# Seven-product projections of a two-layer attention kernel: the fourteen products of a pair in another order

## The chip, the cores and the metric

The kernel runs on one core of a Trainium2 chip. A core has a matrix engine (TensorE, PE in the profile), a vector engine (VectorE, DVE), a scalar engine (ScalarE, ACT), a general engine (GpSimd, POOL) and a queue that issues transfers (SyncE, SP). Each engine works through its own list of instructions in order, and semaphores tie the lists together. Matrix products land in PSUM, a memory of eight banks; a bank holds 512 fp32 values in each of 128 partitions. The metric is the device time of one execution in microseconds (us).

## The reference

Two residual layers run one after the other on `x` of shape 1 x 128 x 256 x 256 (row, position, channel), all in fp32. The part that the change concerns is the four projections of layer 0: q, k, v and the gate, each a product of every row (256 positions x 256 channels) with a 256 x 256 matrix.

```python
# layer 0: x = x + attention(group_norm(x)), for each of 128 rows s, 8 heads of 32 channels
bias = einsum('nijz,zh->nhij', pair_repr, bias_proj)
gate = sigmoid(msa @ gate_proj)
q, k, v = split(msa @ qkv_proj, 3)
sim = softmax(einsum('nsqhc,nskhc->nshqk', q, k) / sqrt(32)) + bias
out = (einsum('nshqk,nskhc->nsqhc', sim, v) * gate) @ out_proj
# layer 1: x = x + banded_attention(group_norm(x)), 4 heads of 64 channels, |i - j| <= 16,
# with biases on its input and output projections
```

## The kernel before

A first stage loads `x` for the statistics of the group norm and turns the pair bias. Layer 0 then goes row by row over `s` from 0 to 128, with the instructions of TensorE, ScalarE and VectorE in exactly the order in which the program text calls them. Layer 1 follows, and the change doesn't touch it.

**Seven products for two rows.** Two neighbouring rows (pair `i`) are projected together. A projection of two rows by a 256 x 256 matrix is a 2 x 2 by 2 x 2 product of blocks of 128, which takes eight block products, or seven with sums of blocks formed beforehand. The kernel uses seven. The sums of weight blocks (`sums_q` and so on) are made once. The sums of input blocks (`ts`) are made on POOL for each pair by `sum_rows`. The class `Seven` (lines 589 to 631) holds one projection: `ps` is its bank in PSUM, with two halves of 256 columns; `to` is the result in SBUF; `mid` holds two partial results.

- Products 1, 6, 7 and 4 go into half 0 of the bank one after the other and add up there, so the half is read between them: after 1, after 6, after 7 and after 4.
- Products 5 and 3 add up in half 1, which is read after 5 and after 3 (the last reading takes both halves, after 3 and 4).
- Product 2 goes to another bank, `twos`, which the two projections of a stretch share.

Each reading is a copy by ScalarE, in `take`: "15" (both halves, 512 columns, line 621), "6" (half 0, 256 columns, line 623), "7" (half 0, line 625) and "34" (both halves, line 627). The copy of `twos` (512 columns, line 756) is the ninth of a stretch. POOL adds the parts together in `add` (lines 630 and 631). On TensorE, q, k and g are products of 256 columns at line 610, v is two products of 128 columns at line 614. Every fp32 product is recorded as two matmuls and two weight loads (four of each for v).

**The stretch.** `stretch(names, i)` does the fourteen products of two projections, f and g: "qk" in even rows and "vg" in odd rows. In the text below, f6 is product 6 of f, and so on. The order on TensorE before is

f1 f5 g1 g5 f2 g2 f6 g6 f3 g3 f7 g7 f4 g4

and the order of the copies on ScalarE is

f15 g15 f6 g6 twos f7 g7 f34 g34.

A product into a bank waits until the last copy out of this bank has ended. A copy waits for the last product into its bank that stands ahead of it in the program.

**Around the stretch.** In a row the order on TensorE is: scores of the first four heads (`sim`, line 640), sums of the heads' weights of the row before (`zs`, 681), products with the bias (`bv`, 667), scores of the other four heads, products `av` of the row before (667), the stretch, and the output projection `po` of the row before (513). `po` waits for `at`, which VectorE computes from `av`, the reciprocal `d` and `bv` (lines 697 to 715). ScalarE takes the exponentials `ex` of the scores (651) and the copies. The banks of `ps`, `twos`, `po` and the scores come from one ring of five.

Of the kernel before, what the change touches and what calls it, by code (L numbers as in the profile page):

```python
# [9 lines left out]
F32 = mybir.dt.float32  # L10
# [5 lines left out]
P = 128  # L16
R = 256
# [22 lines left out]
def conv_preact_kernel(  # L40
# [31 lines left out]
    def bank(which, name):  # L72
        pool, tag, bufs = ring[which]
        return pool.tile([P, 2, R], F32, tag=tag, name=name, bufs=bufs)

    def proj_bank(name):
        return bank("proj", name)
# [461 lines left out]
    with ExitStack() as both:  # L539
# [11 lines left out]
        with ExitStack() as lay0:  # L551
            row = lay0.enter_context(tc.tile_pool(name="row0", bufs=2))
# [179 lines left out]
            def stretch(names, i):  # L732

                if 2 * i >= S:
                    return
                f, g = (Seven(w, i) for w in names)

                f.open()
                f.product(1)
                f.product(5)  # L740
                g.open()
                g.product(1)
                g.product(5)
                f.take("15")
                twos = proj_bank(f"p2{names}{i}")
                f.product(2, twos[:, 0, :])
                g.product(2, twos[:, 1, :])
                g.take("15")
                f.product(6)
                g.product(6)  # L750
                f.take("6")
                f.product(3)
                g.product(3)
                g.take("6")
                two = row.tile([P, 2, R], F32, tag="two", name=f"two{names}{i}")
                nc.scalar.copy(two, twos)  # L756
                f.product(7)
                g.product(7)
                f.take("7")
                g.take("7")  # L760
                f.product(4)
                g.product(4)
                f.take("34")
                g.take("34")
                for n, p in enumerate((f, g)):
                    p.add(two[:, n, :])


            with tc.manual_schedule(engines={mybir.EngineType.PE, mybir.EngineType.Activation, mybir.EngineType.DVE}):
                for s in range(2):  # L770
                    normal(s)
                sum_rows(0)
                stretch("qk", 0)
                for s in range(2, 4):
                    normal(s)
                stretch("vg", 0)
                sum_rows(1)
                for s in range(S + 1):
                    if s < S:
                        scores(s, 0)  # L780
                    zs = sum_heads(s - 1)
                    join_tiles(s, 0, 0)
                    divide(s - 1, zs)
                    if s % 2 == 0 and s < S:
                        e = res["g", s // 2]
                        nc.scalar.activation(e, e, AF.Exp, scale=-1.0)
                    if s < S:
                        scores(s, 1)
                    z = hd[s - 1, "z"][0] if s > 0 else None
                    attend(s - 1)  # L790
                    for half, j in ((0, 2), (1, 0), (1, 2)):
                        join_tiles(s, half, j)
                    least(s - 1, z)
                    if s == S - 1:
                        most1 = join_most(st1, stats1, 1)
                        load1(0)
                        load1(1)
                    stretch(("qk", "vg")[s % 2], s // 2 + 1)
                    normal(s + 4)
                    if s % 2 == 1:  # L800
                        sum_rows((s + 3) // 2)
                    if s > 0:
                        finish(s - 1, by_channel(out_sb, 0, st[s - 1]["at"], f"po{s - 1}"))
# [6 lines left out]
        with ExitStack() as lay:  # L810
            ps_av = psum(lay, "1", 4, 0)
            row = lay.enter_context(tc.tile_pool(name="row1", bufs=4))
# [186 lines left out]
    with tc.If(sure < P):  # L999
        with ExitStack() as lay:  # L1000
            one = lay.enter_context(tc.tile_pool(name="one2", bufs=1))
            two = lay.enter_context(tc.tile_pool(name="two2", bufs=2))
# [174 lines left out]
```

## Time and profile before

| | |
|---|---|
| time, median of 3 runs | 3417.53 us (3411.97 to 3417.85) |
| span of the profiled execution | 3410.0 us |
| TensorE clock granted | 0.992 |
| TensorE matmuls busy | 3292.2 us |
| TensorE weight loads busy | 2476.5 us |
| VectorE busy | 2554.7 us |
| ScalarE busy | 1781.7 us |
| POOL busy | 1140.2 us |
| layer 0's first product, first scores, last output projection | at 193.1, 208.9 and 2228.8 us |
| stretches in layer 0 | 64 "qk" and 64 "vg" |

Layer 0 is thus some 2030 us of the span, or about 15.8 us for a row. Busy times are sums of the lengths of records. Records of matmuls overlap, since a matmul begins before the one before it has ended, so that a busy TensorE is not one that never waits. A weight load (PEld) is recorded by itself and normally runs while the product before it is still at work. In a line of the timeline, the columns are the start, the length, the engine, the line of the kernel, the operation, output and inputs by name, shapes and count; what stands in brackets at the end is how long the engine was idle before it, and what ended that.

### The profile page before, as it was taken

The page shows a single profiled execution, that of the slowest core. Times are in us where ns is not written, and L with a number is a line of the kernel's source. Part 1 is how long each engine was busy: PE and PEld are TensorE (multiplying, and loading weights), DVE is VectorE, ACT ScalarE, POOL GpSimd, SP SyncE. Part 2 cuts the span into 40 slices and gives each one's busy share as a digit, 9 for nine tenths or more (in the row PEclk, how much of TensorE's full clock was granted, in tenths as well). Part 3 has the DMA queues.
Part 4 walks back from the last instruction along what each step waited for, and adds up shares of the span by engine and source line. Part 5 has one row for each costly group of instructions (what it writes and reads, how often), then busy time and mean ns, then how long its engine had stood idle before and what let it go on. Part 6 is the DMA issues. An engine that isn't in the chain of part 4 may idle for free.

```text
span 3410.0 us, 86688 instructions
## 1 busy us (share of the span) xinstructions
PE 3292.2 (97%) x37193; PEld 2476.5 (73%) x37193; DVE 2554.7 (75%) x3794; ACT 1781.7 (52%) x3866; POOL 1140.2 (33%) x1135
## 2 busy tenths in 40 slices
PE   6799999999999999999999999989999999999997
PEld 4466666666666666666666666678888888888886
DVE  4747777787787777778778777757777777777777
ACT  4565555555555556555565555534444444444442
POOL 3033333333333333333333333223333333333332
PEclk9999999999999999999999999999999999999999
DMA  9921111111111111111111111002222222222221
GB/s 383 411 59 52 48 35 32 38 32 32 39 32 38 32 37 33 32 38 32 32 39 32 39 32 32 20 20 64 54 61 64 64 61 54 64 64 63 54 61 46
DMA packets 346328, 209.36 MB, mean 61 GB/s; under 512 B 273608, under 2 KB 339152, under 8 KB 339664
## 3 DMA queue, kind: packets, MB, share of 16 engines
q1 hardware_dynamic: 345040, 201.37, 20.2%
q8 instruction: 294, 4.82, 0.6%
q0 software_dynamic: 752, 2.36, 0.2%
q14 instruction: 98, 0.80, 0.1%
q10 hardware_dynamic: 144, 0.00, 0.0%
HBM read 136.59 MB, written 67.11 MB: 60 GB/s over the span
## 4 chain that ended last, share of the span: by engine, by line
PE 87%; ACT 5%; DMA 3%; DVE 3%; issue 1%; SPq 0%; ACTq 0%; POOL 0%; DVEq 0%
PE sim L640 8%; PE p1v L841 7%; PE av L667 7%; PE 1po L513 7%; PE p1q L513 7%; PE p1k L513 7%; PE po L513 6%; PE bv L667 6%; PE pv L614 6%; PE pq L610 5%; PE pk L610 4%; PE zs L681 4%; DMA xs<-in_x_dram 3%; PE pg L610 3%; PE 1sim L862 3%; PE 1avz L894 2%
## 5 line engine op out<-in xcount | busy, mean ns | idle before, releaser
L651 ACT ACTIVATE ex<-sim 128x512 f32<-128x512 f32 x1024 | 528.8, 603 | 362.9 <-PE sim L640 362.9
L919 DVE RECIPROCAL 1rz<-1z 128x512 f32<-128x512 f32 x128 | 427.6, 3341 | 174.2 <-ACT 1z L917 174.2
L872 POOL TENSOR_TENSOR 1p<-1ex,seen 128x768 f32<-128x768 f32 x128 | 233.4, 1824 | 737.4 <-ACT 1ex L870 737.4
L697 DVE RECIPROCAL d<-d 128x512 f32<-128x512 f32 x128 | 429.2, 3353 | 4.3
L657 DVE TENSOR_TENSOR both<-ex 128x512 f32<-128x512 f32 x512 | 332.8, 690 | 121.4 <-ACT ex L651 121.3
L640 PE MATMUL sim<-q,k 32*128 32x256 f32 x4096 | 294.9, 400 | 1.2 <-ACT ex L651 1.2
L630 POOL TENSOR_TENSOR v<-v,twovg 128x256 f32<-128x256 f32 x64 | 46.6, 728 | 735.7 <-ACT twovg L756 735.7
L833 ACT ACTIVATE 1q<-p1q,bqk 128x256 f32<-128x256 f32 x256 | 107.5, 471 | 345.2 <-PE p1q L513 345.2
L640 PEld LDWEIGHTS sim<-q,k 32*128 32x128 f32 x4096 | 186.2, 184 | 102.3 <-issue 92.8
L513 PE MATMUL po<-at,out_sb 128*128 128x256 f32 x1024 | 245.4, 383 | 12.1 <-DVE at L715 12.1
L667 PE MATMUL av<-ex,v 128*32 128x256 f32 x4096 | 247.5, 382 | 0.0
L513 PE MATMUL 1po<-1at,w_out_t 128*128 128x256 f32 x1024 | 241.9, 389 | 5.1 <-DVE 1at L921 5.1
L513 PE MATMUL p1q<-xn,w_in_t 128*128 128x256 f32 x1024 | 244.1, 381 | 2.0 <-DVE xn L493 1.1
L667 PE MATMUL bv<-bias_sb,v 128*32 128x256 f32 x4096 | 244.5, 379 | 0.0
L513 PE MATMUL p1k<-xn,w_in_t 128*128 128x256 f32 x1024 | 243.2, 381 | 0.0
L841 PE MATMUL p1v<-w_in_t,xn 128*64 128x128 f32 x4096 | 237.9, 274 | 0.0
L841 PEld LDWEIGHTS p1v<-w_in_t,xn 128*64 128x64 f32 x4096 | 222.2, 137 | 21.6 <-issue 21.6
L513 PEld LDWEIGHTS 1po<-1at,w_out_t 128*128 128x128 f32 x1024 | 191.3, 192 | 54.5 <-ACT 1z L917 23.9
L723 DVE TENSOR_TENSOR o<-po,xt 128x512 f32<-128x512 f32 x128 | 88.5, 692 | 187.1 <-PE po L513 186.9
L513 PEld LDWEIGHTS po<-at,out_sb 128*128 128x128 f32 x1024 | 196.4, 192 | 40.6 <-issue 7.7
L630 POOL TENSOR_TENSOR q<-q,twoqk 128x256 f32<-128x256 f32 x64 | 46.6, 728 | 525.3 <-ACT twoqk L756 525.3
L513 PEld LDWEIGHTS p1q<-xn,w_in_t 128*128 128x128 f32 x1024 | 195.3, 191 | 29.4 <-issue 1.3
(226 smaller groups left out, 6722.2 us busy)
## 6 DMA issues: line engine op xcount, KB each, us to landing
pr<-in_L_conv_pair_repr_dram SPq DMA_DIRECT2D x32, 1024.0 KB, 23.0
x<-o SPq DMA_DIRECT2D x64, 512.0 KB, 2.8
yg<-x SPq DMA_DIRECT2D x64, 512.0 KB, 4.2
out_dram<-1o SPq DMA_DIRECT2D x256, 128.0 KB, 4.0
xg<-in_x_dram SPq DMA_DIRECT2D x252, 128.0 KB, 3.2
xs<-in_x_dram SPq DMA_DIRECT2D x15, 2048.0 KB, 21.7
xs<-in_x_dram SPq DMA_DIRECT2D x2, 1024.0 KB, 17.8
qkv_sb<-in_L_conv_qkv_proj_dram POOLq DMA_DIRECT2D x4, 192.0 KB, 12.7
```

What stands on the lines that cost most here:

```text
L513: nc.tensor.matmul(ps[:, m, :], lhsT=w[:, kt, col + m * P : col + (m + 1) * P], rhs=xn[:, kt, :], start=(kt == 0), stop=(kt == 1),)
L610: nc.tensor.matmul(out, lhsT=stationary(self.w, n), rhs=moving, start=first, **flags)
L614: nc.tensor.matmul(out[:, cols], lhsT=moving[:, cols], rhs=stationary(self.w, n), start=first and t2 == 0, **flags)
L640: nc.tensor.matmul(sims[j][:, kt, :], lhsT=k[p0 : p0 + D0, 2 * r + half, kt * P : (kt + 1) * P], rhs=q[p0 : p0 + D0, 2 * r + half, :], sta ...
L651: nc.scalar.activation(ex[:, j], sims[j], AF.Exp, scale=1.0 / math.sqrt(D0))
L657: nc.vector.tensor_tensor(both[:, j : j + 2], ex[:, j : j + 2, 0, :], ex[:, j : j + 2, 1, :], ALU.add)
L667: nc.tensor.matmul(to[D0 * j : D0 * (j + 1), half, :], lhsT=v[:, 2 * r + half, c0 : c0 + D0], rhs=weights(4 * half + j, kt), start=(kt == ...
L681: nc.tensor.matmul(zs[D0 * j : D0 * (j + 1), half, :], lhsT=ones[:, 0:D0], rhs=both[:, j, :], start=True, stop=True,)
L697: nc.vector.reciprocal(d, d)
L841: nc.tensor.matmul(ps[KB * half : KB * (half + 1), b, :], lhsT=xn[:, kt, KB * b : KB * (b + 1)], rhs=w_in_t[:, kt, 2 * C + P * half : 2 * ...
L872: nc.gpsimd.tensor_tensor(p.rearrange("p j (r c) -> p (j r) c", c=WROW)[:, :, 0 : 2 * WSTEP] .rearrange("p r (t c) -> p r t c", c=WSTEP)[: ...
L919: nc.vector.reciprocal(rz, z)
```

## The change

The order of the products and copies within a stretch is changed. Product 3 of each projection goes ahead of product 6, and every copy stands right behind the product whose result it reads. The copy of the twos moves ahead of the copies of product 6, and its tile in SBUF is allocated earlier. The products themselves, the copies, the banks and the additions stay as they are. The order on TensorE after is

f1 f5 g1 g5 f2 g2 f3 f6 g3 g6 f7 g7 f4 g4

and the copies on ScalarE are in the order

f15 g15 twos f6 g6 f7 g7 f34 g34.

It is for this: a copy no longer waits for a product that it doesn't read, and product 3 no longer waits for the copy of product 6, which reads the other half of its bank.

```diff
                 f, g = (Seven(w, i) for w in names)
 
-                f.open()
-                f.product(1)
-                f.product(5)
-                g.open()
-                g.product(1)
-                g.product(5)
-                f.take("15")
+
+                for p in (f, g):
+                    p.open()
+                    p.product(1)
+                    p.product(5)
+                    p.take("15")
                 twos = proj_bank(f"p2{names}{i}")
+                two = row.tile([P, 2, R], F32, tag="two", name=f"two{names}{i}")
                 f.product(2, twos[:, 0, :])
                 g.product(2, twos[:, 1, :])
-                g.take("15")
-                f.product(6)
-                g.product(6)
-                f.take("6")
-                f.product(3)
-                g.product(3)
-                g.take("6")
-                two = row.tile([P, 2, R], F32, tag="two", name=f"two{names}{i}")
                 nc.scalar.copy(two, twos)
-                f.product(7)
-                g.product(7)
-                f.take("7")
-                g.take("7")
-                f.product(4)
-                g.product(4)
-                f.take("34")
-                g.take("34")
+                for p in (f, g):
+                    p.product(3)
+                    p.product(6)
+                    p.take("6")
+                for p in (f, g):
+                    p.product(7)
+                    p.take("7")
+                for p in (f, g):
+                    p.product(4)
+                    p.take("34")
                 for n, p in enumerate((f, g)):
                     p.add(two[:, n, :])
```

## Prediction

> **What bounds the kernel now.** I read the page first: busy shares, then the chain that ended last.
>
> ```profile
> PE 3292.2 (97%) x37193; PEld 2476.5 (73%) x37193; DVE 2554.7 (75%) x3794; ACT 1781.7 (52%) x3866; POOL 1140.2 (33%) x1135
> ...
> PE 87%; ACT 5%; DMA 3%; DVE 3%; issue 1%; SPq 0%; ACTq 0%; POOL 0%; DVEq 0%
> ```
>
> TensorE holds 87% of the chain. Its 97% busy doesn't say that nothing is left: records of matmuls overlap, so short waits hide under them. The record of the weight loads (PEld) has gaps there. The waits of that queue, by what ended them, were read next (us in total, times, longest):
>
> ```profile
> PEld pq L610 <- issue: 34.6, 66, 0.5
> ...
> PEld pv L614 <- ACT midv L623: 31.3, 64, 0.8
> PEld pv L614 <- ACT midv L625: 29.9, 64, 0.5
> PEld pq L610 <- ACT midq L623: 27.6, 64, 0.4
> PEld pk L610 <- ACT midk L623: 27.6, 64, 0.4
> ...
> PEld pg L610 <- ACT midg L623: 17.1, 64, 0.6
> ```
>
> Six groups of about 64, one for each stretch, all in the function under change; 168 us gross. Last I read the timeline of one "qk" stretch, f = q and g = k (start, length; x2 is one product, which is recorded as two matmuls):
>
> ```profile
> 1508.45 0.59 PE L610 MATMUL pq<-ts,sums_q 128*128 128x256 f32 x2
> ...
> 1508.88 0.59 PE L610 MATMUL pk<-ts,sums_k 128*128 128x256 f32 x2
> 1509.08 0.37 ACT L623 COPY midq<-pq 128x256 f32<-128x256 f32 x1 [0.71 <-PE pq L610]
> ...
> 1509.51 0.70 PE L610 MATMUL pq<-xn,sums_q 128*128 128x256 f32 x2
> ...
> 1510.04 0.59 PE L610 MATMUL pk<-xn,sums_k 128*128 128x256 f32 x2
> ...
> 1510.47 0.59 PE L610 MATMUL pq<-ts,sums_q 128*128 128x256 f32 x2
> 1510.67 0.37 ACT L623 COPY midk<-pk 128x256 f32<-128x256 f32 x1 [1.22 <-PE pk L610]
> 1510.94 0.59 ACT L756 COPY twoqk<-p2qk 128x512 f32<-128x512 f32 x1
> ...
> 1511.10 0.70 PE L610 MATMUL pk<-ts,sums_k 128*128 128x256 f32 x2
> 1511.42 0.39 ACT L625 COPY midq<-pq 128x256 f32<-128x256 f32 x1
> ...
> 1511.96 0.67 PE L610 MATMUL pq<-ts,sums_q 128*128 128x256 f32 x2 [0.16 <-ACT midq L625]
> ```
>
> These are f6, g6, (copy of f6), f3, g3, f7, (copy of g6, copy of the twos), g7, (copy of f7), f4. The copy of g6 starts only at 1510.67, right after g3 and long after g6: it stands behind g3 in the program and waits for it.
>
> **Prices from this timeline.** Undisturbed products start 0.433 us apart (1506.29, 1506.72, 1507.16, 1507.59). A copy starts 0.63 after the product it waits for (1508.45 to 1509.08); it takes 0.37, the copy of a product 7 of f 0.39, one of 512 columns 0.59, and the next copy can start 0.10 to 0.12 before that ends (1510.94 to 1511.42). A product held by a copy really starts 0.16 after the copy's end: 1509.45 to 1509.61, where I put its start 0.10 later than recorded because its record is 0.70 long and not 0.59. A held product with a second wait (POOL) starts 0.23 after it (1511.81 to 1512.04). So a turn of product, copy, next product in the same bank needs 0.63 + 0.37 + 0.16 = 1.16, for f4 1.25. One product in between gives 0.87: a stall of 0.30. Two give 1.30: none.
>
> **What the Trainium skill says.** "PSUM — Partial Sum Buffer", section "PSUM bank collisions raise a hardware error": guard by bank and quadrant, not by address. The trace agrees: f3 writes the other half of the bank than the copy of f6 reads, and still starts 0.06 after that copy ends. So moving 3 ahead of 6 removes a wait that the bank, not the data, imposes. "ScalarE: Activation LUTs", section "What ACT_TABLE_LOAD costs": 186 ns + 0.833 ns per column, neighbours overlapping by 93 ns; 399 and 613 ns for 256 and 512 columns, against 372 and 586 to 592 here; I use the trace's. "Perfetto Trace Analysis", section "Identifying Dependency Chains": a second wait may become an instruction of its own ahead; the 0.23 against 0.16 is its price here.
>
> **The change, part by part.** It adds no instruction and removes none: 14 products and 9 copies stay. Before, the waits cost in a qk stretch: f3 for the copy of f6, 0.30; g7 for the copy of g6, which started after g3 (g3, f7, g7 leave 0.87 of 1.16), 0.30; f4 for the copy of f7, held on ScalarE by the copies of g6 and the twos (1511.42 where the product alone would allow 1511.10), 0.41. Sum 1.01. Check: f1 starts at 1505.86, the projection po at 1512.89, 7.03, less 14 x 0.433 = 6.06, leaves 0.97. The vg stretch at 1016.96 to 1024.13: 7.17 less 14 x 0.437 leaves 1.05.
>
> After, f1 at 0: f5 0.43, g1 0.87, g5 1.30, f2 1.73, g2 2.17, f3 2.60, f6 3.03, g3 3.46, g6 3.90. The build's order of waits shows f3 and g3 waiting for the copies of f5 and g5 alone, which end at 0.43 + 0.63 + 0.59 = 1.65 and 2.52: no stall. The copy of the twos now runs from 2.80 to 3.39 and is out of ScalarE's way when the copy of f6 starts at 3.66 (to 4.03). f7, with two waits, could start at 4.26 and has its slot at 4.33: no stall, with 0.07 in hand. Copy of g6 4.53 to 4.90, g7 at 5.06 for a slot at 4.76: stall 0.30. Copy of f7 4.96 to 5.35, f4 at 5.58 for a slot at 5.49: 0.09. Copy of g7 5.69 to 6.06, g4 at 6.22 for 6.01: 0.21. po at 6.65. So 0.60 is left and 0.38 to 0.39 gained. The same sum for vg, where the copies of product 6 start 0.07 later (two waits) and v4 has one, gives po at 6.75: 0.42 gained. 64 x (0.385 + 0.42) = 51.5 us.
>
> Behind these products on TensorE stand po and the next row's scores, and nobody else is queued. The scores reuse the banks of f, g and twos; the last copy ends at 7.4 and they start at po + 1.82 = 8.5. The earlier additions on POOL cost nothing: POOL is 33% busy and q, k feed the row after next. Whether VectorE keeps up is shown by a row without a stretch near the end, where po waits for it:
>
> ```profile
> 2198.01 1.93 PE L667 MATMUL av<-ex,v 128*32 128x256 f32 x32
> 2203.32 1.97 PE L513 MATMUL po<-at,out_sb 128*128 128x256 f32 x8 [3.38 <-DVE at L715]
> ```
>
> VectorE has `at` ready 5.3 us after the products av begin; with a stretch po comes after 9.0 now (1503.89 to 1512.89) and 8.6 then. 3.3 us of slack remain, so the gain isn't given back there.
>
> Unknown: the hand-over to f7 has only 0.07 in hand, and the prices carry some 0.05 each. If each of f7, g7, f4, g4 took 0.05 more, a stretch loses 0.2, 128 x 0.2 = 26 us: 3392. If the copies started or ended enough sooner to shorten g7's and g4's turns by 0.07 each, 18 us more are gained: 3348. I take the sum as worked out.
>
> **Rivals.**
> 1. Part of the gain is lost: f7 misses its slot as it did before (0.15), and VectorE or POOL, whose operations now overlap others, take 0.05. 0.2 of 0.4 is left, 26 us: 3392. For it: f7's small margin. Against: the slack of 3.3 us.
> 2. Nothing changes: the wait moves from f3 to f7 whole. Then f7 would stall by 0.4, so the copy of f6 would have to come 0.4 late; ScalarE is idle for 0.27 before it. 3417.
> 3. All waits go, 1.01 x 128 = 129 us: 3288. Against: g7 and g4 still have only one product between.
> 4. Slower: had f3 to wait for the copy of the twos too, which now stands ahead of it on ScalarE's queue, it would start at 3.55 and not 2.60; 0.95 - 0.40 lost, 128 x 0.55 = 70 us: 3488. For it: that copy was moved forward and every wait on ScalarE counts its instructions in order. Against: the build gives f3 the count of the copy of f5, two copies earlier. A lower clock under denser work is the other way to lose; layer 1 has PEld busy 493 of 560 us at clock 0.99, layer 0 535 of 794 at 1.00, so no.
>
> **How the numbers follow.** Forecast 0.80, rival 1 0.08, 2 0.03, 3 0.03, 4 with the clock 0.06. Time 3417.5 - 51.5 = 3366. The range 3346 to 3390 takes both ends of the unknown prices. Faster by over 0.2%: 0.80 + 0.08 + 0.03 = 0.91; same 0.03; slower 0.06.
>
> **What would show it.** Right: the waits of weight loads for midq and midv at product 3 (31.3 and 27.6 us) gone; the waits before g7 stay near 0.4 each in the record; new ones of the same size before g4; none, or below 0.1, before f7; the copy of the twos directly ahead of the copy of f6; f1 to po 6.6 to 6.8 us. Wrong: f7's load waiting for midq in every stretch, or po waiting for `at`.

## The result, and the profile after

The changed kernel takes 3362.49 us (median of 4 runs, 3361.67 to 3366.80); the kernel before took 3414.81 us beside it (4 runs, 3411.97 to 3417.85). The ratio is 0.9849, with a 95% interval of 0.9832 to 0.9866: 52 us gained, where 51.5 was forecast. The profiled execution spans 3361.1 us against 3410.0.

Busy time of the engines and the shares of the chain that ended last, from the page of the changed kernel:

```profile
PE 3268.2 (97%) x37193; PEld 2493.9 (74%) x37193; DVE 2685.3 (80%) x3794; ACT 1818.2 (54%) x3866; POOL 1254.2 (37%) x1135
...
PE 92%; DMA 4%; DVE 2%; ACT 1%; issue 0%; ACTq 0%; SPq 0%; POOL 0%; DVEq 0%
```

The same number of instructions, and the same 97% for TensorE: that share tells nothing of what happened, as it told nothing of the waits before. What changed is the chain. ScalarE held 5% of it and holds 1%: TensorE's path leads over fewer copies. Two numbers went the wrong way. VectorE is busy 131 us longer (2554.7 before) and POOL 114 us (1140.2), with as many instructions as before. The forecast had neither; its rival 1 names an overlap, at 0.05 us a stretch. It is taken up below. ScalarE's 37 us more (1781.7 before) are not longer copies: those of 256 columns take 372 to 374 ns (372 to 390 before), those of 512 columns 585 to 588 (586 to 593). A busy time here counts overlapping records once, so it is less than the sum of their lengths, and the copies of the stretches now overlap less.

The waits of the weight-load queue in the changed kernel (us in total, times, longest):

```profile
PEld pk L610 <- ACT midk L623: 27.6, 64, 0.4
...
PEld pk L610 <- ACT midk L625: 23.5, 64, 0.4
...
PEld pg L610 <- ACT midg L623: 16.8, 64, 0.3
...
PEld pg L610 <- ACT midg L625: 13.3, 64, 0.2
PEld pq L610 <- issue: 12.9, 64, 0.3
```

Of the six groups shown of before, the copies of f6 (midq and midv at line 623, 27.6 and 31.3 us) no longer hold a product, nor does the copy of v7 (midv at 625, 29.9). The copies of g6 (midk and midg at 623) hold g7 as before, 27.6 and 16.8 against 27.6 and 17.1. The group put down to "issue", which holds f4 in qk, fell from 34.6 to 12.9. New are the copies of g7 (midk at 625, 23.5, and midg at 625, 13.3), which hold g4. No copy holds f7.

One qk stretch of the changed kernel, from its timeline (start, length; x2 is one product), in the order f6, copy of the twos, g3, POOL's first addition, copy of f6, g6, f7, copy of g6, g7, copy of f7, f4, copy of g7, g4, and `po` behind:

```profile
1508.54 0.59 ACT L748 COPY twoqk<-p2qk 128x512 f32<-128x512 f32 x1 [0.28 <-PE p2qk L610]
...
1508.77 0.59 PE L610 MATMUL pq<-ts,sums_q 128*128 128x256 f32 x2
...
1509.20 0.59 PE L610 MATMUL pk<-xn,sums_k 128*128 128x256 f32 x2
1509.20 1.15 POOL L630 TENSOR_TENSOR q<-q,twoqk 128x256 f32<-128x256 f32 x1 [4.90 <-ACT twoqk L748]
1509.40 0.37 ACT L623 COPY midq<-pq 128x256 f32<-128x256 f32 x1 [0.28 <-PE pq L610]
...
1509.63 0.59 PE L610 MATMUL pk<-ts,sums_k 128*128 128x256 f32 x2
...
1510.07 0.59 PE L610 MATMUL pq<-ts,sums_q 128*128 128x256 f32 x2
1510.27 0.37 ACT L623 COPY midk<-pk 128x256 f32<-128x256 f32 x1 [0.49 <-PE pk L610]
...
1510.69 0.70 PE L610 MATMUL pk<-ts,sums_k 128*128 128x256 f32 x2
1510.70 0.37 ACT L625 COPY midq<-pq 128x256 f32<-128x256 f32 x1
...
1511.23 0.66 PE L610 MATMUL pq<-ts,sums_q 128*128 128x256 f32 x2
1511.43 0.37 ACT L625 COPY midk<-pk 128x256 f32<-128x256 f32 x1 [0.36 <-PE pk L610]
...
1511.85 0.70 PE L610 MATMUL pk<-ts,sums_k 128*128 128x256 f32 x2
...
1512.39 0.38 PE L513 MATMUL po<-at,out_sb 128*128 128x256 f32 x1
```

Read it as turns. The copy of f6 starts 0.63 after f6 and ends at 1509.77; f7 starts at 1510.07, in its own slot, 0.44 after g6. The copy of g6 ends at 1510.64 and g7 starts 0.16 after it in truth (1510.80; its record of 0.70 begins 0.10 early), 0.30 behind its slot. g4 follows the copy of g7 in the same way. f1 starts in truth at 1505.74, `po` at 1512.39: 6.65 us, as worked out. In vg it is 6.77 (6.75 worked out).

From `po` to the f1 of the next stretch it is 8.57 us before (1512.89 to 1521.46 recorded) and after (1512.39 to 1520.95: 8.56), so nothing is given back there. Two rows, from one f1 of qk to the next, take 31.54 us before and 30.74 after (median over layer 0); 0.795 x 64 = 51 us. Layer 1 takes nearly the same (its products from first to last `po` 1114.4 and 1115.6 us).

### The profile page after: what moved, and what is told of

The parts are those of the page before. It is cut to its first block, busy times and chain, and to the rows that moved or that the text cites. A ratio compares the mean times of both kernels' runs of the same rounds, so it can differ in the third digit from the quotient of the medians.

```text
span 3361.1 us, 86626 instructions
## 1 busy us (share of the span) xinstructions
PE 3268.2 (97%) x37193; PEld 2493.9 (74%) x37193; DVE 2685.3 (80%) x3794; ACT 1818.2 (54%) x3866; POOL 1254.2 (37%) x1135
## 4 chain that ended last, share of the span: by engine, by line
PE 92%; DMA 4%; DVE 2%; ACT 1%; issue 0%; ACTq 0%; SPq 0%; POOL 0%; DVEq 0%
PE sim L640 8%; PE p1v L835 7%; PE av L667 7%; PE 1po L513 7%; PE po L513 7%; PE p1q L513 7%; PE p1k L513 7%; PE bv L667 6%; PE pg L610 6%; PE pk L610 6%; PE pq L610 5%; PE pv L614 5%; PE zs L681 4%; PE 1sim L856 3%; PE 1avz L888 2%; DMA xs<-in_x_dram 2%
## 5 line engine op out<-in xcount | busy, mean ns | idle before, releaser
L657 DVE TENSOR_TENSOR both<-ex 128x512 f32<-128x512 f32 x512 | 463.1, 944 | 113.0 <-ACT ex L651 113.0
L630 POOL TENSOR_TENSOR v<-v,twovg 128x256 f32<-128x256 f32 x64 | 56.7, 886 | 592.8 <-ACT twovg L748 592.8
L513 PEld LDWEIGHTS p1k<-xn,w_in_t 128*128 128x128 f32 x1024 | 194.6, 190 | 26.5
L493 DVE TENSOR_SCALAR xn<-yg,mean,rstd 128x256 f32<-128x256 f32 x256 | 94.0, 410 | 138.7 <-PE p1v L835 138.7
```

The source lines that it names most:

```text
L513: nc.tensor.matmul(ps[:, m, :], lhsT=w[:, kt, col + m * P : col + (m + 1) * P], rhs=xn[:, kt, :], start=(kt == 0), stop=(kt == 1),)
L657: nc.vector.tensor_tensor(both[:, j : j + 2], ex[:, j : j + 2, 0, :], ex[:, j : j + 2, 1, :], ALU.add)
```

## The experiments

Theory: all that the stretch loses are the turns product, copy, next product in the same bank, as the prediction summed them; so any other order can be summed in the same way, and work placed inside a slack turn is free. Rivals: one half of the change does all of it; VectorE, POOL or something else outside the stretch limits what can be gained; the gain hangs on how much work ScalarE does and not on where it stands. Each kernel was timed in 5 rounds beside the kernel before. That took 3417.80 us beside the two parts of the change, both fillers and the swapped additions, 3416.73 beside the extra copies, one filler and POOL in order, and 3417.55 beside both fillers with POOL in order and the changed kernel run again, which took 3363.85 (ratio 0.9843, 0.9829 to 0.9856). Diffs are against the changed kernel unless the text says otherwise. No kernel leaves out any of the computation.

Lengths from f1 to `po` hardly vary within a run (a few vg stretches take up to 0.3 us longer), so they are read from one stretch. Two places outside the stretches do vary between executions: the first microseconds of layer 0, and the rows behind its last stretch, of which more at the end. From the `po` of the last stretch to the last `po` these rows take 40.6 us in the profile of the changed kernel, 42.0 in that of the same kernel run again, and 43.3 in four of the kernels below.

### Parts of the change alone

Copies moved, product 3 still behind product 6:

```diff
                 for p in (f, g):
-                    p.product(3)
                     p.product(6)
                     p.take("6")
+                for p in (f, g):
+                    p.product(3)
```

> The copies alone are moved: product 6 stays ahead of 3 as in the kernel before, and every copy stands right behind its product, the copy of the twos behind g2. Theory (every stall is a turn of product, copy, next product of 1.16 us less the slots of the products in between): in qk f3 stalls 0.35, f4 0.39, g3, g7 and g4 not, f1 to po is 6.8 us; in vg 6.78; 0.24 and 0.39 a stretch gained over the kernel before, 40 us in all, 3375. Rival 1 (the wait of product 3 that the bank imposes is what counts): f3 still waits, so the time is that of the kernel before, 3415. Rival 2 (the late release of the copy of g6 is all): 3362.

Measured: 3375.73 us, ratio 0.9877 (0.9862 to 0.9892), a gain of 42. f1 to `po` 6.76 in qk (1511.90 to 1518.66) and 6.79 in vg. Its waits show which turn is left:

```profile
PEld pq L610 <- ACT midq L623: 31.2, 64, 0.5
PEld pv L614 <- ACT midv L623: 31.0, 64, 0.5
PEld pq L610 <- POOL k L630: 30.1, 61, 0.5
PEld pv L614 <- ACT midv L625: 27.4, 64, 0.4
```

f3 again waits for the copy of f6, and pays for it; f4 waits for the copy of f7. In qk the record puts f4's wait down to POOL's addition, which ends 0.06 later than that copy. But f4 starts in truth 0.23 after the end of the copy (1517.81 and 1517.58), as it did in the kernel before, so the copy is what it waits for. g3 and g7 now have enough between.

The other part, product 3 ahead of 6, with the copy of the twos behind the copies of product 6 as before:

```diff
-                nc.scalar.copy(two, twos)
                 for p in (f, g):
                     p.product(3)
                     p.product(6)
                     p.take("6")
+                nc.scalar.copy(two, twos)
```

> Product 3 goes ahead of 6 as in the changed kernel, but the copy of the twos stays behind the copies of product 6 as in the kernel before. Theory: the copy of the twos holds the copy of f7 by 0.3 on ScalarE, f4 stalls 0.4 in place of 0.09 and g4 then no longer 0.2; f1 to po is 6.75 in qk and 6.78 in vg against 6.65 and 6.77 in the changed kernel; 6 us slower than it, 3369. Rival (the early copy of the twos is a large part of the gain): half of the gain gone, 3390.

Measured: 3374.17 us, ratio 0.9870 (0.9855 to 0.9886), a gain of 44; f1 to `po` 6.74 and 6.82. The stretches of a pair are 0.14 longer than in the changed kernel, 9 us in all, or 3371. The other 3 us, and so most of the miss against the 3369 written down, lie behind the last stretch in the profile: 43.3 us against 40.6. From its timeline, the copy of the twos, g7, the copies of f7 and g7, and f4:

```profile
1516.04 0.59 ACT L752 COPY twoqk<-p2qk 128x512 f32<-128x512 f32 x1
1516.20 0.70 PE L610 MATMUL pk<-ts,sums_k 128*128 128x256 f32 x2
1516.52 0.39 ACT L625 COPY midq<-pq 128x256 f32<-128x256 f32 x1
1516.93 0.37 ACT L625 COPY midk<-pk 128x256 f32<-128x256 f32 x1
1517.05 0.67 PE L610 MATMUL pq<-ts,sums_q 128*128 128x256 f32 x2 [0.16 <-ACT midq L625]
```

f7 started at 1515.57, so its copy could have begun at 1516.20; the twos ahead of it on ScalarE hold it until 1516.52, and f4 pays. So neither part is the change: they gain 42 and 44 us, and the whole 54. The two gains can't be added, for the parts aren't disjoint: in both, the copies, but for that of the twos in the second, stand right behind their products. The copies as they stood before, with product 3 ahead, weren't run. That saved stalls don't add up is seen from the second part to the whole change, where the products stand in the same order. f4's stall falls from 0.40 to under 0.1, but g4, which did not wait, now stalls by 0.22, and only 0.10 is gained in qk. A stall gives a later turn time for free, and saving it lets the later one appear.

### The same added work in two places

If the sum of turns is right, a copy more on ScalarE costs a full turn where the next product waits, and nothing where there is slack. An extra copy of 256 columns was added ahead of the copy of product 6, first for g (k and g), then for f (q and v); its target is overwritten later.

```diff
                     elif what == "6":
+                        if self.w in "kg":
+                            nc.scalar.copy(self.to[:, 2, :], self.ps[:, 1, :])
                         nc.scalar.copy(self.mid[:, 0, :], self.ps[:, 0, :])
```

> The changed kernel with one more copy of 256 columns on ScalarE in every stretch, right ahead of the copy of g6 and from the same bank (its result is overwritten later). The copy of g6, and with it the turn from g6 to g7, gets 0.27 us longer in qk and 0.21 in vg. Theory: g7 already waits for this turn, so the whole delay reaches the end of the stretch (f1 to po 6.92 in place of 6.65 in qk): 128 x 0.24 = 31 us slower than the changed kernel, 3393. Rival (ScalarE is 54% busy and has room for it): 3362.

Measured: 3397.54 us, ratio 0.9945 (0.9930 to 0.9959), 34 us over the changed kernel. The extra copy (line 624), the copies of g6 and f7, and g7:

```profile
1501.66 0.37 ACT L624 COPY k<-pk 128x256 f32<-128x256 f32 x1 [0.49 <-PE pk L610]
1501.92 0.38 ACT L625 COPY midk<-pk 128x256 f32<-128x256 f32 x1
1502.19 0.39 ACT L627 COPY midq<-pq 128x256 f32<-128x256 f32 x1
...
1502.36 0.70 PE L610 MATMUL pk<-ts,sums_k 128*128 128x256 f32 x2 [0.30 <-ACT midk L625]
```

A copy adds 0.26 here, since neighbours overlap, and g7 waits that much longer. The stretches are 0.27 (qk) and 0.22 (vg) longer than in the changed kernel: 31 us over 64 pairs, as expected. The other 3 lie behind the last stretch (43.3 us against 40.6).

The same copy for f, as a diff against the kernel above:

```diff
-                        if self.w in "kg":
+                        if self.w in "qv":
```

> The same extra copy, but ahead of the copy of f6. The turn from f6 to f7 becomes longer than its three slots, and f7 starts 0.2 us late. Theory: the end of the stretch is set by g6, g7 and g4, whose turns don't begin later for it: f7's delay uses up the time that g7 waits anyway, f4 starts 0.18 later and g4 then has its 0.2 of waiting filled; f1 to po stays 6.65: 3362, within 0.3%. Rival (every longer copy costs what it adds, or f7's 0.2 stays): 25 to 31 us slower, 3387 to 3393.

Measured: 3367.27 us, ratio 0.9856 (0.9840 to 0.9872): 3 to 5 us over the changed kernel's medians, with intervals that overlap. Two rows take 30.74 us, as in the changed kernel. The extra copy, the copy of f6, f7, the copy of g6, and g7:

```profile
1509.19 0.37 ACT L624 COPY q<-pq 128x256 f32<-128x256 f32 x1 [0.28 <-PE pq L610]
...
1509.46 0.38 ACT L625 COPY midq<-pq 128x256 f32<-128x256 f32 x1
1509.98 0.67 PE L610 MATMUL pq<-ts,sums_q 128*128 128x256 f32 x2
1510.06 0.37 ACT L625 COPY midk<-pk 128x256 f32<-128x256 f32 x1 [0.22 <-PE pk L610]
1510.49 0.69 PE L610 MATMUL pk<-ts,sums_k 128*128 128x256 f32 x2
```

The copy of f6 ends at 1509.84, 1.28 after f6 against 1.00 in the changed kernel, and f7 now misses its slot: 1510.06 in truth for 1509.85. But the copy of g6 isn't delayed, and g7 starts in truth at 1510.59, 5.05 after f1 as in the changed kernel (5.06): what f7 loses, the wait before g7 no longer has to take. In eight of the 64 vg stretches, though, 246 us apart, the copy of g6 starts later than its product asks, and g7 waits for it:

```profile
356.28 0.37 ACT L625 COPY midg<-pg 128x256 f32<-128x256 f32 x1 [0.55 <-PE pg L610]
...
PEld pg L610 <- ACT midg L625: 3.2, 8, 0.4
```

The copy starts 0.97 after g6 there, where it is 0.69 in the other vg stretches, and the stretch is 0.28 longer: 2 us in all. Why it starts late the trace doesn't show. The rest again lies behind the last stretch (43.3 us). So the same 128 copies cost the stretches 31 us in one place and 2 in the other. The rival that counts ScalarE's work, whatever its place, is out.

### Filling the short turns

Product 2 of f and g goes to a bank of its own and depends on no copy of the stretch: it can stand where a turn lacks a product. First one of the two, g2 between f7 and g7:

```diff
                 f.product(2, twos[:, 0, :])
-                g.product(2, twos[:, 1, :])
-                nc.scalar.copy(two, twos)
...
-                for p in (f, g):
-                    p.product(7)
-                    p.take("7")
+                f.product(7)
+                f.take("7")
+                g.product(2, twos[:, 1, :])
+                nc.scalar.copy(two, twos)
+                g.product(7)
+                g.take("7")
```

> Only product 2 of g is moved, between f7 and g7: f1 f5 g1 g5 f2 f3 f6 g3 g6 f7 g2 g7 f4 g4. Theory: g7 and f4 have two products ahead of them since their predecessors and stall no longer; g4 still has one and stalls 0.3; f1 to po is 6.36 in qk and 6.40 in vg: 0.33 a stretch gained on the changed kernel, 42 us, 3320. Rival (moving a stall only hands it on): 3362.

Measured: 3331.16 us, ratio 0.9752 (0.9738 to 0.9766). 31 us under the changed kernel and 11 above what was expected; f1 to `po` 6.40 and 6.49 instead of 6.36 and 6.40. The timeline shows what the sum had missed, the copy of the twos between the copies of f7 and g7:

```profile
1517.88 0.59 PE L610 MATMUL pk<-ts,sums_k 128*128 128x256 f32 x2
1518.09 0.59 ACT L754 COPY twoqk<-p2qk 128x512 f32<-128x512 f32 x1
1518.32 0.59 PE L610 MATMUL pq<-ts,sums_q 128*128 128x256 f32 x2
1518.57 0.38 ACT L625 COPY midk<-pk 128x256 f32<-128x256 f32 x1
...
1519.00 0.70 PE L610 MATMUL pk<-ts,sums_k 128*128 128x256 f32 x2
```

g7 started at 1517.88 and its copy could have at 1518.51; the twos let it start at 1518.57. g4 starts 0.06 later for it, and `po` with it: that covers the 0.04 of qk. In vg the same delay is 0.05 (1533.72 for 1533.67), and its eleven slots up to g7 take 4.84 where 0.437 each makes 4.81, so 0.08 of the 0.09 is found. Over 64 pairs the two are 8 of the 11 us. The lesson is in the ScalarE queue: a filler brings its own copy, and that copy has to stand somewhere.

Then both, f2 between f7 and g7 and g2 between f4 and g4, so that the order is f1 f5 g1 g5 f3 f6 g3 g6 f7 f2 g7 f4 g2 g4:

```diff
-                f.product(2, twos[:, 0, :])
-                g.product(2, twos[:, 1, :])
-                nc.scalar.copy(two, twos)
...
-                for p in (f, g):
-                    p.product(7)
-                    p.take("7")
-                for p in (f, g):
-                    p.product(4)
-                    p.take("34")
+                f.product(7)
+                f.take("7")
+                f.product(2, twos[:, 0, :])
+                g.product(7)
+                g.take("7")
+                f.product(4)
+                f.take("34")
+                g.product(2, twos[:, 1, :])
+                nc.scalar.copy(two, twos)
+                g.product(4)
+                g.take("34")
```

> The two products 2, which wait for nothing, are put where the changed kernel still stalls: f1 f5 g1 g5 f3 f6 g3 g6 f7 f2 g7 f4 g2 g4, so that two products stand between every product and its successor in the bank. Theory: only f3 stalls (0.07), f1 to po is 6.14 in qk and 6.2 in vg against 6.65 and 6.77; 0.54 a stretch gained, 69 us, 3293, if VectorE keeps up. Rival 1 (VectorE, 86% busy in layer 0 of the changed kernel, becomes the bound): 3320 to 3362. Rival 2 (the twos come too late for POOL, and the gate's exponential waits for its sum ahead of the scores' on ScalarE): no gain, 3362 or more.

Measured: 3298.59 us (3296.82 to 3301.12), ratio 0.9649 (0.9636 to 0.9662): 119 us under the kernel before and 64 under the changed one, the shortest order tried. f1 to `po` is 6.13 in qk and 6.23 in vg, where fourteen slots alone are 6.06 and 6.12. The stretches gain 68 us on the changed kernel where 69 were expected; most of the 5 us by which the time misses the 3293 lies in the two places outside them, the start of layer 0 and the rows behind the last stretch (42.3 us). From its waits:

```profile
PEld pv L614 <- ACT v L621: 13.6, 64, 0.2
...
PEld pq L610 <- ACT q L621: 13.2, 62, 0.2
```

With the twos gone from their old place, f3 has two products before it and the copy of 512 columns: 0.63 + 0.59 + 0.16 = 1.38 for 1.30. That 0.08 is the last turn that costs. The prediction's rival 3, all waits gone at 3288, is thus nearly to be had, by another order.

### The longer VectorE and POOL

In the changed kernel VectorE's additions of exponentials (line 657) and POOL's additions of the twos (line 630) last longer than before. Groups of the kernel before (busy, mean ns of one, idle before):

```profile
L657 DVE TENSOR_TENSOR both<-ex 128x512 f32<-128x512 f32 x512 | 332.8, 690 | 121.4 <-ACT ex L651 121.3
L723 DVE TENSOR_TENSOR o<-po,xt 128x512 f32<-128x512 f32 x128 | 88.5, 692 | 187.1 <-PE po L513 186.9 <-PE bv L667 0.2
```

Those of the changed kernel:

```profile
L657 DVE TENSOR_TENSOR both<-ex 128x512 f32<-128x512 f32 x512 | 463.1, 944 | 113.0 <-ACT ex L651 113.0
L723 DVE TENSOR_TENSOR o<-po,xt 128x512 f32<-128x512 f32 x128 | 87.6, 685 | 52.8 <-PE po L513 52.6 <-PE bv L667 0.2
```

And its additions of the twos on POOL, 728 and 734 ns of one before:

```profile
L630 POOL TENSOR_TENSOR k<-k,twoqk 128x256 f32<-128x256 f32 x64 | 74.1, 1158 | 0.0
L630 POOL TENSOR_TENSOR q<-q,twoqk 128x256 f32<-128x256 f32 x64 | 72.1, 1127 | 309.7 <-ACT twoqk L748 309.7
```

Counted from f1, the twos are copied 2.3 us earlier (2.80 against 5.08), so POOL adds them from 1509.20 on, where VectorE has its three additions from 1509.08 on. The Trainium skill, "SBUF — State Buffer", section "Who interferes with whom", says that a VectorE instruction with two inputs in SBUF contends with a GpSimd instruction that reads SBUF, since its second input comes over a read interface which the two share. The trace agrees: both sides grow where they overlap, from 690 to 944 and from 728 to 1127 ns. In the kernel with product 3 ahead and the twos copied late they don't: 709 and 727 to 729 ns. VectorE's wait for `po`, its slack, shrank from 187 to 53 us.

Does it cost time? Two kernels were to put the twos' additions last. The first swaps the two lines of `add`:

```diff
                 def add(self, two):
-                    nc.gpsimd.tensor_tensor(self.to[:, 0], self.to[:, 0], two, ALU.add)
                     nc.gpsimd.tensor_tensor(self.to[:, 2:4], self.to[:, 2:4], self.mid, ALU.add)
+                    nc.gpsimd.tensor_tensor(self.to[:, 0], self.to[:, 0], two, ALU.add)
```

> The changed kernel with POOL's two additions for a projection in the other order: the partial results first, the twos last, so that POOL starts after the last copies and no longer while VectorE joins the tiles of exponentials. Theory: the longer VectorE joins (944 ns against 690 in the kernel before) and POOL additions (1150 ns against 730) of the changed kernel come from running beside each other, and TensorE doesn't wait for either: VectorE's busy time falls from 2685 to some 2560 us, the join to 690 ns, and the time stays within 0.2% of 3362. Rival: the slower VectorE takes part of the gain, and without it the time is 3340 to 3352.

Measured: 3362.04 us, ratio 0.9838 (0.9825 to 0.9852). It answers nothing: POOL's order isn't taken from the program text, and in the trace the twos were still added first (additions of exponentials 945 ns). The second swaps the lines and takes POOL's order from the text too:

```diff
-            with tc.manual_schedule(engines={mybir.EngineType.PE, mybir.EngineType.Activation, mybir.EngineType.DVE}):
+            with tc.manual_schedule(engines={mybir.EngineType.PE, mybir.EngineType.Activation, mybir.EngineType.DVE, mybir.EngineType.Pool}):
```

> The changed kernel with POOL's instructions too in the order of the program text, where they were placed by the planner, and each projection's partial results added first, the twos last; so POOL starts on a stretch only after its last copies. (In the run with the additions swapped alone the planner had put the twos first all the same, so nothing had changed.) Theory: VectorE's joins and POOL's additions take longer in the changed kernel because they run at the same time, and TensorE doesn't wait for them: the joins go from 945 to some 690 ns, VectorE's busy time from 2685 to some 2560 us, the time stays within 0.2% of 3362. Rival: the slower VectorE takes part of the gain: 3340 to 3352.

Measured: 3362.62 us, ratio 0.9846 (0.9832 to 0.9860). Its groups:

```profile
L657 DVE TENSOR_TENSOR both<-ex 128x512 f32<-128x512 f32 x512 | 361.1, 746 | 121.9 <-ACT ex L651 121.9
...
L723 DVE TENSOR_TENSOR o<-po,xt 128x512 f32<-128x512 f32 x128 | 88.5, 692 | 220.7 <-PE po L513 220.7
```

VectorE is busy 2503.5 us, 182 less than in the changed kernel, its slack before `po` is 221 us (187 in the kernel before), and the time is the same. Of the 182 the additions give 102, at 746 ns where 690 were expected; the normalization of rows (`xn`, line 573), from 705 to 398 ns, gives 79. So the longer operations are real and free here: they eat slack that nobody waits for. The same was done to the order with both fillers, to see whether it is still free with shorter stretches:

> The order with both products 2 as fillers, and POOL in the order of the program text with the twos added last. The run with the fillers alone took 3298.6 where the turns gave 3293. Theory: the 5 us are not VectorE's or POOL's, since the stretch to po and from po to the next stretch have their lengths in its trace; the same time within 0.2%, 3298, with VectorE's busy time lower by 150 us or more. Rival (VectorE at 88% of layer 0 holds something up in the run with the fillers): 3293 or less.

Measured: 3296.78 us (3296.18 to 3301.07), ratio 0.9648 (0.9635 to 0.9662), the time of the fillers without it, as expected. The other half of the expectation failed: VectorE is busy 2663.6 us, against 2655.8 with both fillers and POOL's order free. Its additions take 743 ns (773), but the normalization of rows 1080 ns (919), which took 398 in the kernel above: the lengthening has moved to another instruction. The same section of the Trainium skill, "SBUF — State Buffer", "Who interferes with whom", counts `tensor_scalar`, which this is, among the instructions that can contend with GpSimd where their operands meet certain conditions. That it is the same contention is argued from there and not shown; no kernel took it apart. Little slack is left in these orders: VectorE waits 21 us in total for `po` with both fillers and 10 with POOL in order too.

## Why the prediction was right

**The bound.** TensorE's queue with the waits of weight loads was the right view. All of the gain lies in the stretches: 0.395 (qk) and 0.40 (vg) from f1 to `po` in the profile, where 0.385 and 0.42 were forecast, with `po` to the next f1 unchanged.

**The turn.** Its price of 1.16 (0.63 + 0.37 + 0.16) held in the changed kernel and carried over to four other orders (copies only, order only, one filler, two), f1 to `po` within 0.04 us of the sum but for one (vg with one filler, 0.09 off). With the extra copy for g, qk came out at the 6.92 of the sum. f7's margin of 0.07, the weakest step, held. The second wait, for which the prediction takes 0.07 more, has its own record: ahead of f4's weight load in the kernel before stands an EVENT_SEMAPHORE of 0.05 us. (That f3 starts 0.06 after the copy of f6 is read from its record there; by the prediction's own price it really starts 0.16 after.)

**The waits named ahead.** Gone at product 3, kept at g7, new at g4, none at f7, copy of the twos directly ahead of that of f6: all as written. The waits at g4 were to be of the size of those at g7, and are for qk. For vg the wait is smaller in the record of weight loads (13.3 us in total against 23.5 for qk), though the product g4 itself starts 0.29 behind its slot; the stretch is still 6.77.

**The rivals.** None came. No wait stands before f7 (rivals 1 and 2), f3 doesn't wait for the twos (4), and g7 and g4 kept their waits (3). One reading in rival 1 was wrong: f7 did not miss its slot before, but follows g3 by 0.43 in the stretch shown. VectorE and POOL "whose operations now overlap others" did overlap, by far more than the rival priced, and took nothing.

**What was off.** "The earlier additions on POOL cost nothing: POOL is 33% busy" came to the right cost by a wrong reason. POOL's share of busy time said nothing of what its additions do to VectorE, whose busy time rose by 131 us. What kept that free is the slack of VectorE, which the prediction had read for another purpose (3.3 us a row before) and which was then largely used. A kernel with less of it would have paid.

**Sizes.** 51 us from the stretches, 49 between the profiled executions, 52 to 54 between medians. Executions of the kernel before lie near 3412 or near 3417 us, and the profiled one, at 3411.7, is among the short ones, which can account for the three us between 49 and 52. The forecast of 51.5 is close to the 51 of the stretches by its sum, whose errors in qk and vg (0.01 too little, 0.02 too much) are small and cancel in part. That it lies 1 us from the medians too is in part luck, since single executions differ by more.

## What to carry to other kernels

Where a matrix engine and a copying engine share a bank, take the price of one turn from the timeline and count the slots of independent work between two uses of that bank; in the orders tried here, a turn cost what it lacked in slots, and the copying engine's load said nothing. Saved stalls don't add up: after removing one, sum the whole sequence again, since the next turn may have been living on it. Products that depend on no copy are best kept for the turns that lack one, and a long copy of theirs must not stand ahead of a short one that the next product awaits.

## What the runs showed of the hardware

Two-input additions on VectorE and additions on POOL slow each other where they overlap: 690 to 944 ns and 728 to 1127 ns as means over the kernel, for the same instructions on the same sizes.

TensorE's clock at the start of layer 0 isn't the same in every execution. From 195 to 240 us it was 1.00 in the profile of before and 0.94 in that of the changed kernel, whose first product took 1.06 us recorded against 0.60, and whose first scores came at 211.2 us against 208.9 although its order is shorter. With both fillers it was 0.86. From 240 us to 1115 us it was 1.00 in both.

The rows behind the last stretch of layer 0 differ too. They take 40.6 us at a mean clock of 0.88 in the changed kernel, 42.0 at 0.88 when it is run again, 42.3 at 0.85 with both fillers, and 43.3 at 0.82 or 0.83 with copies only, order only and either extra copy. The work in these rows is the same in all of them, and the mean clock goes with their length only roughly. Each of the two places moves single executions by 2 or 3 us, so differences below 5 us between medians are read here only where the stretches show them; what decides the clock there wasn't tried.
